# Where the second layer norm is applied, and how modulation weight rows are grouped, in an adaLN block with a long convolution

## The chip, the cores and the metric

One Trainium2 chip, one of its cores. The engines of a core run side by side, each through its own instructions in order: TensorE (PE in the profile, with its weight loads as PEld), VectorE (DVE), ScalarE (ACT), GpSimd (POOL) and SyncE (SP), whose queue issues nearly all DMAs here. The metric is the device time of one execution in microseconds; 2164.45 is the median of three runs.

## What is computed

A block on x of shape (4, 1024, 2048): a modulation vector, a layer norm with scale and shift, a long causal convolution along the last axis with a kernel from a state-space model, a gated residual, a second layer norm with its own scale and shift, and a linear layer with a low-rank update, gated again.

```python
mod = (_silu(L0_c) @ L0_wmod).reshape(L0_c.shape[0], 6, 1, -1)
sa, ca, ga, sb, cb, gb = (mod[:, 0], mod[:, 1], mod[:, 2], mod[:, 3], mod[:, 4], mod[:, 5])
ga = (2 * (ga >= 0) - 1) * jnp.maximum(jnp.abs(ga), 0.25)
gb = (2 * (gb >= 0) - 1) * jnp.maximum(jnp.abs(gb), 0.25)
h = _layernorm(x, axis=-1) * (1 + ca) + sa
x = x + ga * _L0_attn_ref(h, ...)      # causal convolution over 2048 points, plus D * h
h = _layernorm(x, axis=-1) * (1 + cb) + sb
x = x + gb * _L0_ffn_ref(h, ...)       # h W^T + bias + sum over 16 of w_e (h A_e^T) B_e^T
```

`L0_wmod` is 2048 x 12288, the FFN's W is 2048 x 2048, and A and B have rank 16 for each of 16 experts.

## The kernel before

The 4096 rows of x are worked in 32 tiles of 128 rows ("rows" r = 0 to 31 below) and, in the FFN, in 16 units u of two tiles each. All of x fits only tile by tile, so results between the stages go through HBM.

**Modulation.** The weight matrix of the modulation is cut into six sections of 2048 columns, a section into 16 weight rows of 1 MB (`mod_load`), each followed by four products of 32 output columns (`mod_mm`, L317; f32, so eight matmul records in the profile). Sections 1 and 0 run first, then section 2 (the first gate) beside rows 0 and 1; sections 4, 3 and 5 are filler later. `section` loads and multiplies one row at a time from a pool of three buffers (`WM`).

**Convolution rows.** For each row: `stats` (L497) and `conv_prep` (normalise L514, 16 transposes L535 in groups of four, scale and shift on ScalarE L538, split into two half-precision parts L546 and L547), `conv_mm` (108 half-precision products L567 with ScalarE and VectorE work at its ends, L580 to L594) and `conv_post`. `conv_post` stores the row y to HBM (`x1d`), takes the squares on ScalarE (L614), makes the reciprocal deviation (`rstd`), normalises y on VectorE (L617), transposes it in four groups of four (L623), copies each group out of PSUM on ScalarE (L624) and stores it to HBM (`n2d`, L625).

**Filler.** `PLAN` gives, for ten points in a row's products, what is taken from generators: `P` a step of `conv_post` of the row before, `N` a step of the next row's `conv_prep`, `S` a step of the filler, `T` and `F` the statistics and preparation of row r + 2. There are nine `S` in a row. The filler (`rest`) merges the low-rank update into W, in eight chunks of 15 steps (`merge`: products L443, sums L445, then seven half-precision pieces through L470 and L471), and after every `MR` = 2 merge steps takes one step of the modulation sections 4, 3 and 5. The first merge needs operands made by `prep_lora` (`lbh` and `lbl`, L418 and L419).

**FFN.** The product of a 256 x 2048 unit with a 2048 x 1024 part of W is made by a seven-product scheme of 128 x 1024 by 1024 x 512 blocks (Strassen-like; `ORDER` names the products), each as 24 matmuls (L704) on half-precision pairs. There are two passes q over the 16 units, one for each half of the columns. In pass 0 the function `left` makes the seven left operands of the next unit: it loads the transposed normalised unit from `n2d` (L652), applies scale `cb` and shift `sb` on ScalarE (L654), forms sums on VectorE (L671), casts and takes the remainder (L664, L665) and stores the pairs to HBM (`lfd`, L666); in pass 1 (q = 1) they are loaded again. `ffn_unit` evacuates the accumulators X, Y and Z between the products (copies p1, p5, p6, p7 on ScalarE L712, sums on VectorE), adds the residual from `x1d` (L719, L720) and stores the output (L751). Z is used by three products, so its copies p6 and p7 have to be made before the next one writes it.

What sets the order: the tile framework schedules instructions within the order and the priorities that the generators give; on each engine and on SP's DMA queue they then run strictly in order, and an instruction that waits keeps all behind it.

Of the kernel before, what the change touches and what calls it, by code (L numbers as in the profile page):

```python
# [24 lines left out]
P = 128  # L25
D = 2048
# [8 lines left out]
class Net:  # L35
# [254 lines left out]
    def prep_mod(self, pool):  # L290
        nc, v = self.nc, self.nc.vector
        self.small = pool.tile([P, 265], F32, tag="small", name="small")
        nc.sync.dma_start(out=self.small, in_=self.io["small"])
        c = self.small[:, 201:265].rearrange("p (b j) -> p b j", j=16)
        th = pool.tile([P, NB, 16], F32, tag="mth", name="mth")
        nc.scalar.activation(th, c, AF.Tanh, scale=0.5)
        v.tensor_scalar(th, th, 0.5, 0.5, MUL, ADD)
        v.tensor_tensor(th, th, c, MUL)
        self.sct = self.const("sct", [P, 16, 8, NB])
        v.tensor_copy(  # L300
            self.sct.rearrange("p j r b -> p r b j"),
            th.unsqueeze(1).to_broadcast([P, 8, NB, 16]),
        )
# [20 lines left out]
    def mod_column(self, pool, name, plus_one):  # L324

        nc, v = self.nc, self.nc.vector
        row = pool.tile([P, 512], F32, tag="mg0", name="mrow")
        nc.scalar.copy(row, self.modps)
        ps = self.tps.tile([P, 4, P], F32, tag="t", name="mtp")
        for c in range(4):  # L330
            nc.tensor.transpose(ps[:, c, :], row[:, ds(P * c, P)], self.ident)
        col = self.const(name, [P, NC, NB])
        src = ps.rearrange("p c (q r) -> p q c r", r=32)[:, :, :, 0:NB]
        dst = col.rearrange("p (q c) b -> p q c b", c=4)
        v.tensor_scalar(dst, src, plus_one, None, ADD)
        return col
# [270 lines left out]
    def conv_post(self, pl, r, y, sums):  # L607
        nc, v = self.nc, self.nc.vector
        STQ(nc).dma_start(out=self.x1d[r], in_=y)
        mn = pl["sm"].tile([P, 1], F32, tag="mn", name="mn")  # L610
        v.tensor_scalar(mn, sums[:, 0:1], sums[:, 1:2], -1.0 / D, ADD, MUL)
        n = pl["n"].tile([P, D], F32, tag="n", name="n2")
        sq = pl["sm"].tile([P, 1], F32, tag="sq", name="sq")
        nc.scalar.activation(n, y, AF.Square, bias=mn, accum_out=sq)  # L614
        rs = pl["sm"].tile([P, 1], F32, tag="rs2", name="rs2")
        self.rstd(pl["sm"], sq, rs, 1, "r2", 1.0 / D)
        v.tensor_scalar(n, y, mn, rs, ADD, MUL)  # L617
        yield
        for c0 in range(0, NC, 4):
            nt = pl["nt"].tile([P, 4, P], F32, tag="nt", name="nt")  # L620
            tp = self.tps.tile([P, 4, P], F32, tag="t", name="tp2")
            for k in range(4):
                nc.tensor.transpose(tp[:, k], n[:, ds(P * (c0 + k), P)], self.ident)  # L623
            nc.scalar.copy(nt, tp)  # L624
            NTQ(nc).dma_start(out=self.n2d[r // 2][:, c0 : c0 + 4, r % 2, :], in_=nt)  # L625
            yield
# [18 lines left out]
    def left(self, pl, u):  # L645
        nc, v = self.nc, self.nc.vector
        b = u // 4
        t = pl["t"].tile([P, NC, 2, P], F32, tag="t", name="gt")
        for q in range(4):
            for h in range(2):  # L650
                sl = slice(HC * h + 2 * q, HC * h + 2 * q + 2)
                nc.sync.dma_start(out=t[:, sl], in_=self.n2d[u][:, sl])  # L652
                for c in range(sl.start, sl.stop):
                    nc.scalar.activation(  # L654
                        t[:, c], t[:, c], AF.Identity,
                        bias=self.sb[:, c, b : b + 1], scale=self.cb[:, c, b : b + 1],
                    )
        a11, a12 = t[:, 0:HC, 0, :], t[:, HC:NC, 0, :]
        a21, a22 = t[:, 0:HC, 1, :], t[:, HC:NC, 1, :]
        res = {}  # L660

        def put(i, s):
            hl = pl["l"].tile([P, HC, 2, P], F16, tag="l", name="lf")
            nc.scalar.copy(hl[:, :, 0, :], s)  # L664
            v.tensor_tensor(hl[:, :, 1, :], s, hl[:, :, 0, :], SUB)  # L665
            STQ(nc).dma_start(out=self.lfd[u, i], in_=hl)  # L666
            res[i] = hl

        def comb(x, y, op, tag):
            t = pl["s"].tile([P, HC, P], F32, tag=tag, name=tag)  # L670
            v.tensor_tensor(t, x, y, op)  # L671
            return t

        put(0, a11)
        s1 = comb(a21, a22, ADD, "s1")
        put(4, s1)
        s2 = comb(s1, a11, SUB, "s2")
        put(5, s2)
        put(1, a12)
        put(6, comb(a11, a21, SUB, "s1"))  # L680
        put(2, comb(a12, s2, SUB, "s1"))
        put(3, a22)
        return res
# [9 lines left out]
    def ffn_unit(self, pl, u, q, lf, wc):  # L693
# [21 lines left out]
        xs = []  # L715
        for r in range(2):
            x = pl["o"].tile([P, 2, 512], F32, tag="o", name="xo")
            src = self.x1d[2 * u + r].rearrange("p (h n) -> p h n", h=2)[:, :, ds(512 * q, 512)]
            nc.sync.dma_start(out=x, in_=src)  # L719
            v.tensor_tensor(x, x, self.gbias, ADD)  # L720
            xs.append(x)

        def finish(r, h, cv):
            t = pl["e"].tile([P, 512], F32, tag="fin", name="fin")
            v.tensor_tensor(t, cv, self.gbt[:, h], MUL)
            v.tensor_tensor(xs[r][:, h], xs[r][:, h], t, ADD)
# [3 lines left out]
        p1 = copy("X", "p1")  # L730
        prod(4, "Y")
        p5 = copy("Y", "p5")
        prod(5, "Z")
        p6 = copy("Z", "p6")
        prod(1, "X")
        finish(0, 0, ps["X"])
        v.tensor_tensor(p6, p6, p1, ADD)
        prod(6, "Z")
# [3 lines left out]
        finish(1, 1, p7)  # L742
        prod(2, "Y")
        v.tensor_tensor(p6, p6, ps["Y"], ADD)
        finish(0, 1, p6)
        prod(3, "Z")
        v.tensor_tensor(p1, p1, ps["Z"], ADD)
        finish(1, 0, p1)
        for r in range(2):
            dst = self.io["out"][ds(256 * u + P * r, P), :].rearrange("p (h n) -> p h n", h=2)[:, :, ds(512 * q, 512)]  # L750
            STQ(nc).dma_start(out=dst, in_=xs[r])  # L751
# [5 lines left out]
MR = 2  # L757
ACC, TPS = 5, 2
PLAN = ("PNS", "N", "NS", "NT", "PS", "PS", "PS", "PS", "FS", "SS")
R0 = 3  # L760
WM, WMS = 3, 3
# [14 lines left out]
def net(ctx: ExitStack, tc: tile.TileContext, io):  # L776
# [5 lines left out]
    k.n2d = k.dram.tile([NU, P, NC, 2, P], F32, tag="n2d", name="n2d")  # L782
# [13 lines left out]
    def section(sec, pools):  # L796
        for q in range(16):
            if q == 0:
                k.mod_begin()
            k.mod_mm(k.mod_load(pools[q % len(pools)], sec, q), q)  # L800
            yield
        if sec == 0:
            k.sa = k.mod_column(msm, "sa", 0.0)
            k.hinv = k.fold_scale(msm, k.ca, k.sa, "fs1")
        elif sec == 1:
            k.ca = k.mod_column(msm, "ca", 1.0)
        elif sec == 2:
            k.gas, (k.gad,) = k.mod_gate(msm, "gad")
        elif sec == 4:
            k.cb = k.mod_column(msm, "cb", 1.0)  # L810
        elif sec == 3:
            k.sb = k.mod_column(msm, "sb", 0.0)
        else:
            _, k.gbd = k.mod_gate(msm, "gbd", io["bias"])
        yield
# [26 lines left out]
    for sec in (1, 0):  # L842
        for _ in section(sec, (wms, wmp)):
# [10 lines left out]
    for name, bufs in (("h", 2), ("n", 2), ("t", 2), ("y", 2), ("g", 1), ("nt", 2)):  # L854
        pl[name] = pool(left, "p1" + name, bufs)
    def rest():
        mods = (x for sec in (4, 3, 5) for x in section(sec, (wmp,)))
# [30 lines left out]
    def early():  # L888
        right.close()
        for name, bufs in (("w", 1), ("l", 8), ("t", 1), ("s", 1)):  # L890
            pr[name] = pool(p2, "p2" + name, bufs, "right")
        load_w(0, ORDER[0])

# [13 lines left out]
    sec = section(2, (wmp,))  # L907
# [3 lines left out]
    take(sec, 16)  # L911
# [9 lines left out]
    k.conv_late(xs.pop(0), *ys[0])  # L921
    take(k.conv_post(pl, 0, *ys[0]), 9)
    k.conv_late(xs.pop(1), *ys[1])
    post = k.conv_post(pl, 1, *ys[1])
    for r in range(2, 32):
# [6 lines left out]
        if r == LEFT0:  # L932
            while "w" not in pr:
                step()
            lf[0] = k.left(pr, 0)
# [3 lines left out]
        def tick():  # L939
            for a in next(plan):  # L940
                if a == "S":
                    step()
                elif a == "P":
                    take(post, 1)
# [8 lines left out]
        y = k.conv_mm(pl, hs.pop(r), xs.pop(r), tick, False)  # L953
        tick()
        take(post, 9)
        take(nxt, 9)
        post = k.conv_post(pl, r, *y)
        nxt = follow[0] if follow else iter(())
    take(post, 9)
    left.close()  # L960

    for name in ("v", "o", "e", "g"):
        pr[name] = pool(p2l, "p2" + name, 3 if name == "o" else 1)
    for q in range(2):
# [5 lines left out]
        for u in range(NU):  # L970
# [10 lines left out]
            k.ffn_unit(pr, u, q, lf.pop(u), wc)  # L981
            if u + 1 < NU:
                lf[u + 1] = (k.left if q == 0 else k.left_again)(pr, u + 1)
# [55 lines left out]
```

## Time and profile before

| | |
|---|---|
| three runs | 2163.26, 2164.45, 2166.11 us |
| the profiled execution: its run, its span | 2165.34 us, 2163.6 us |
| PE busy | 2080.5 us (96%) |
| DVE busy | 1355.8 us (63%) |
| ACT busy | 938.8 us (43%) |
| DMA traffic | 516.62 MB, mean 239 GB/s |
| TensorE clock granted, mean | 0.984 |

The span runs from the first to the last instruction of the program. Busy times of an engine are unions of its records; matmuls are pipelined, so a record is longer than the slot that it takes, and the distance from start to start tells more than the length. In the profile's lines `out<-in` names the tiles, L704 is line 704 of the kernel, and the last columns of a group are busy time, mean length of one and the idle time ahead of it with what ended it. Until about 110 us the kernel loads and multiplies modulation weights and builds the convolution's kernel; the rows end at 987 us, the first FFN pass at about 1577 us.

### The profile page before, as it was taken

How to read it: one execution, taken by the hardware profiler on the slowest of the kernel's cores; microseconds unless marked ns; L12 is line 12 of the kernel's file. 1: busy time of each engine (PE TensorE's matmuls, PEld its weight loads, DVE VectorE, ACT ScalarE, POOL GpSimd, SP SyncE). 2: the span in 40 equal slices, each digit the busy share in tenths (PEclk: the TensorE clock that was granted, in tenths of full speed). 3: DMA queues.
4: the chain of work that ended last, by engine and by line, in shares of the span. 5: the costliest groups of instructions: out<-in, count | busy, mean ns of one | idle time of the engine just before them, and what ended most of it. 6: DMA issues, size and time to landing. Idle time of an engine off the chain costs nothing.

```text
span 2163.6 us, 28506 instructions
## 1 busy us (share of the span) xinstructions
PE 2080.5 (96%) x11084; PEld 1019.0 (47%) x11084; DVE 1355.8 (63%) x2293; ACT 938.8 (43%) x1795; POOL 2.8 (0%) x12
## 2 busy tenths in 40 slices
PE   5698999999999999999999999999999999999998
PEld 1144555555555555564444444444444444444443
DVE  6538798889989999964665766666533333232333
ACT  1057677767776779862453535454200000000000
POOL 0000000000000000000000000000000000000000
PEclk8799999999999999999999999999999999999999
DMA  9988597888787657648756565656785544544541
GB/s 393 371 284 299 197 333 272 303 317 294 277 294 281 244 207 246 220 163 307 246 218 230 215 241 209 239 201 241 289 329 180 185 154 174 166 171 160 176 155 68
DMA packets 206497, 516.62 MB, mean 239 GB/s; under 512 B 15206, under 2 KB 80871, under 8 KB 179479
## 3 DMA queue, kind: packets, MB, share of 16 engines
q1 hardware_dynamic: 205824, 513.21, 66.3%
q8 instruction: 87, 1.43, 0.3%
q10 hardware_dynamic: 538, 1.59, 0.2%
q14 instruction: 48, 0.39, 0.1%
HBM read 325.89 MB, written 188.85 MB: 238 GB/s over the span
## 4 chain that ended last, share of the span: by engine, by line
PE 63%; DVE 15%; DMA 10%; ACT 9%; issue 2%; SPq 1%; POOL 0%; DVEq 0%; ACTq 0%
PE fZ L704 19%; PE fY L704 12%; PE fX L704 11%; PE ya L567 8%; PE yb L567 4%; PE modps L317 3%; DMA gt<-n2d 3%; PE lps L443 2%; ACT gt L654 2%; DVE lf L665 2%; PE tp L623 2%; ACT t L538 2%; ACT n L614 2%; DMA wm<-in_wmod 1%; DMA xo<-x1d 1%
## 5 line engine op out<-in xcount | busy, mean ns | idle before, releaser
L704 PEld LDWEIGHTS <-lf 128*128 128x128 f16 x5376 | 526.3, 98 | 643.0 <-issue 11.5
L704 PE MATMUL fZ<-w,lf 128*128 128x512 f16 x2304 | 514.8, 380 | 6.7 <-ACT p L712 6.7
L704 PE MATMUL fX<-w,lf 128*128 128x512 f16 x1536 | 342.6, 379 | 0.0
L704 PE MATMUL fY<-w,lf 128*128 128x512 f16 x1536 | 342.5, 379 | 0.0
L567 PEld LDWEIGHTS <-hc 128*128 128x128 f16 x2304 | 215.8, 98 | 190.7 <-issue 34.7
L720 DVE TENSOR_TENSOR xo<-xo,gb 128x1024 f32<-128x1024 f32 x64 | 78.4, 1224 | 207.0 <-DMA xo<-x1d 198.6
L538 ACT ACTIVATE t<-tp,sa,ca 128x128 f32<-128x128 f32 x512 | 199.6, 466 | 10.2 <-DVE sa L376 4.7
L654 ACT ACTIVATE gt<-gt,sb,cb 128x256 f32<-128x256 f32 x256 | 132.7, 592 | 151.7 <-DMA gt<-n2d 151.6
L567 PE MATMUL ya<-kh,hc 128*128 128x512 f16 (+3 forms) x768 | 192.6, 326 | 1.8 <-ACT qs L580 1.8
L567 PE MATMUL ya<-kh,hs 128*128 128x512 f16 (+3 forms) x768 | 193.3, 327 | 0.5 <-ACT hs L546 0.3
L567 PE MATMUL yb<-kh,hc 128*128 128x512 f16 (+3 forms) x768 | 193.0, 326 | 0.0
L317 PE MATMUL modps<-wm,sct 128*32 128x512 f32 x768 | 123.5, 687 | 32.2 <-DMA wm<-in_wmod 23.1
L567 PEld LDWEIGHTS <-hs 128*128 128x128 f16 x1152 | 107.6, 98 | 98.0 <-issue 17.7
L712 ACT COPY p<-fZ 128x512 f32<-128x512 f32 x64 | 37.3, 582 | 256.6 <-PE fZ L704 256.6
L712 ACT COPY p<-fX 128x512 f32<-128x512 f32 x32 | 18.5, 578 | 267.8 <-PE fX L704 254.9
L567 PE MATMUL ya<-kl,hs 128*128 128x512 f16 (+3 forms) x384 | 125.4, 326 | 0.0
L567 PE MATMUL yb<-kl,hc 128*128 128x512 f16 (+3 forms) x384 | 125.4, 326 | 0.0
L567 PE MATMUL ya<-kl,hc 128*128 128x512 f16 (+3 forms) x384 | 125.1, 326 | 0.0
L664 ACT CAST lf<-s 128x1024 f16<-128x1024 f32 x64 | 67.2, 1049 | 105.1 <-DVE s L671 78.7
L624 ACT COPY nt<-tp 128x512 f32<-128x512 f32 x128 | 74.9, 594 | 62.9 <-PE tp L623 43.3
L547 DVE TENSOR_TENSOR hc<-t,hc 128x512 f16<-128x512 f32 x128 | 87.5, 684 | 9.7 <-ACT hc L546 9.7
L535 PE MATMUL tp<-ident,n 128*128 128x128 f32 x512 | 79.4, 279 | 13.1 <-ACT t L538 11.6
(236 smaller groups left out, 2227.2 us busy)
## 6 DMA issues: line engine op xcount, KB each, us to landing
wm<-in_wmod SPq DMA_DIRECT2D x96, 1024.0 KB
lfd<-lf SPq DMA_DIRECT2D x112, 512.0 KB
lf<-lfd SPq DMA_DIRECT2D x112, 512.0 KB
x<-in_x SPq DMA_DIRECT2D x32, 1024.0 KB
x1d<-y SPq DMA_DIRECT2D x32, 1024.0 KB
n2d<-nt SPq DMA_DIRECT2D x128, 256.0 KB
gt<-n2d SPq DMA_DIRECT2D x128, 256.0 KB
xo<-x1d SPq DMA_DIRECT2D x64, 512.0 KB
```

The costliest lines, as they stand in the source:

```text
L317: self.last = self.nc.tensor.matmul(self.modps[32 * g : 32 * g + 32, :], self.sct[:, j].rearrange("p r b -> p (r b)"), w[:, ds(512 * g, 512)],
L443: nc.tensor.matmul(ps, la[:, x, k, h], y[:, k, osl], start=(n == 0), stop=(n == 5))
L535: nc.tensor.transpose(tp[:, k], n[:, ds(P * (c0 + k), P)], self.ident)
L538: nc.scalar.activation(t[:, k], tp[:, k], AF.Identity, bias=self.sa[:, c, b : b + 1], scale=self.ca[:, c, b : b + 1],)
L547: v.tensor_tensor(lo[:, sl], src, hi[:, sl], SUB)
L567: nc.tensor.matmul(pf[:, o:512], h, self.kf[f][z][:, ds(k0, 512 - o)], start=first, stop=(i == last and (x, z) == (1, 0)), skip_group_chec ...
L624: nc.scalar.copy(nt, tp)
L654: nc.scalar.activation(t[:, c], t[:, c], AF.Identity, bias=self.sb[:, c, b : b + 1], scale=self.cb[:, c, b : b + 1],)
L664: nc.scalar.copy(hl[:, :, 0, :], s)
L704: nc.tensor.matmul(ps[name], lf[i][:, k, x, :], wc[i][k // 4][:, k % 4, y, :], start=(first and n == 0), stop=(n == 3 * HC - 1), skip_grou ...
L712: nc.scalar.copy(t, ps[name])
L720: v.tensor_tensor(x, x, self.gbias, ADD)
```

## The change

**The layer norm.** `conv_post` no longer normalises, transposes or stores `n2d`. It keeps two numbers a row in a constant tile, `ln2`: the reciprocal deviation and minus the mean times it. Its square activation writes into the row's x tile instead of a tile of its own. In the FFN's first pass `left` loads the two rows of its unit from `x1d` (1 MB each), normalises them on ScalarE in place, transposes them on PE in eight groups of four, and applies scale and shift on ScalarE straight from PSUM. `left` is now a generator; `LPLAN` takes its steps at seven points, one after each product of `ffn_unit`: two groups of transposes after each of the first four products, the seven puts after the fifth, the loads and normalisation of the unit after next after the sixth. Unit 0 is prepared in rows 30 and 31.

**The modulation.** The last four sections that run (2, 4, 3, 5) load two weight rows and then multiply both; the pool has four buffers instead of three. The filler takes a modulation step after every four merge steps instead of two.

**Around them.** The residual is loaded and the output stored in quarters (128 x 512) instead of halves (128 x 2 x 512), with five buffers instead of three; sums of `left` are made in place; some constants move to pools that end earlier.

```diff
-    def conv_post(self, pl, r, y, sums):
+    def conv_post(self, pl, r, x, y, sums):
...
-        nc.scalar.activation(n, y, AF.Square, bias=mn, accum_out=sq)
-        rs = pl["sm"].tile([P, 1], F32, tag="rs2", name="rs2")
+        nc.scalar.activation(x, y, AF.Square, bias=mn, accum_out=sq)
+        rs = self.ln2[:, r, 1:2]
         self.rstd(pl["sm"], sq, rs, 1, "r2", 1.0 / D)
-        v.tensor_scalar(n, y, mn, rs, ADD, MUL)
-        yield
-        for c0 in range(0, NC, 4):
-            nt = pl["nt"].tile([P, 4, P], F32, tag="nt", name="nt")
-            tp = self.tps.tile([P, 4, P], F32, tag="t", name="tp2")
-            for k in range(4):
-                nc.tensor.transpose(tp[:, k], n[:, ds(P * (c0 + k), P)], self.ident)
-            nc.scalar.copy(nt, tp)
-            NTQ(nc).dma_start(out=self.n2d[r // 2][:, c0 : c0 + 4, r % 2, :], in_=nt)
-            yield
+        v.tensor_tensor(self.ln2[:, r, 0:1], mn, rs, MUL)
...
-    def left(self, pl, u):
+    def left(self, pl, u, res):
         nc, v = self.nc, self.nc.vector
         b = u // 4
+        xs = []
+        for r in range(2):
+            x = pl["x2"].tile([P, D], F32, tag=f"x2{r}", name="x2")
+            nc.sync.dma_start(out=x, in_=self.x1d[2 * u + r])
+            nc.scalar.activation(
+                x, x, AF.Identity, bias=self.ln2[:, 2 * u + r, 0:1], scale=self.ln2[:, 2 * u + r, 1:2]
+            )
+            xs.append(x)
+        yield
         t = pl["t"].tile([P, NC, 2, P], F32, tag="t", name="gt")
-        for q in range(4):
-            for h in range(2):
-                sl = slice(HC * h + 2 * q, HC * h + 2 * q + 2)
-                nc.sync.dma_start(out=t[:, sl], in_=self.n2d[u][:, sl])
-                for c in range(sl.start, sl.stop):
-                    nc.scalar.activation(
-                        t[:, c], t[:, c], AF.Identity,
-                        bias=self.sb[:, c, b : b + 1], scale=self.cb[:, c, b : b + 1],
-                    )
+        for c0 in range(0, NC, 2):
+            tp = self.tps.tile([P, 2, 2, P], F32, tag="t", name="tp2")
+            for c in range(2):
+                for r in range(2):
+                    nc.tensor.transpose(tp[:, c, r], xs[r][:, ds(P * (c0 + c), P)], self.ident)
+            for c in range(2):
+                nc.scalar.activation(
+                    t[:, c0 + c], tp[:, c], AF.Identity,
+                    bias=self.sb[:, c0 + c, b : b + 1], scale=self.cb[:, c0 + c, b : b + 1],
+                )
+            yield
...
-MR = 2
+MR = 4
-PLAN = ("PNS", "N", "NS", "NT", "PS", "PS", "PS", "PS", "FS", "SS")
+PLAN = ("PNSL", "NL", "NSL", "NTL", "SL", "SL", "SL", "SL", "FSL", "SSL")
+LPLAN = ("LL", "LL", "LL", "LL", "L", "0", "")
-WM, WMS = 3, 3
+WM, WMS = 4, 3
...
-    def section(sec, pools):
-        for q in range(16):
-            if q == 0:
-                k.mod_begin()
-            k.mod_mm(k.mod_load(pools[q % len(pools)], sec, q), q)
+    def section(sec, n, pools):
+        k.mod_begin()
+        for q in range(0, 16, n):
+            ws = [k.mod_load(pools[j % len(pools)], sec, j) for j in range(q, q + n)]
+            for j, w in enumerate(ws):
+                k.mod_mm(w, q + j)
             yield
...
-        mods = (x for sec in (4, 3, 5) for x in section(sec, (wmp,)))
+        mods = (x for sec in (4, 3, 5) for x in section(sec, 2, (wmp,)))
...
+            plan = iter(LPLAN)
+            def tick():
+                if q == 1:
+                    return
+                for a in next(plan):
+                    if a == "0":
+                        gens[0] = next_left(u + 2)
+                    take(gens[0], 1)
+            k.ffn_unit(pr, u, q, lf.pop(u), wc, tick)
```

## The prediction

> **What bounds the kernel now.** I read three views, in this order: busy time by stretches of the span, the timeline of TensorE (PE), and the groups of instructions. The stretches first (microseconds, then busy time and instruction count of PE, weight loads, VectorE, ScalarE and GpSimd, then granted clock, DMA share and GB/s):
>
> ```profile
> 200.00:300.00 100.00, 91.14 (x558) 49.22 (x559) 85.27 (x172) 77.03 (x154) 0.54 (x1) 0.97 0.73 256
> 300.00:712.00 412.00, 407.19 (x2582) 221.42 (x2581) 361.66 (x708) 298.29 (x602) 0.00 (x0) 1.00 0.82 291
> 712.00:790.00 78.00, 74.91 (x470) 44.24 (x468) 74.44 (x146) 59.66 (x124) 0.38 (x1) 1.00 0.59 206
> 790.00:987.00 197.00, 189.87 (x1234) 116.89 (x1232) 166.12 (x336) 147.70 (x324) 0.00 (x0) 1.00 0.62 213
> 987.00:1577.00 590.00, 582.77 (x2695) 263.89 (x2693) 363.18 (x408) 254.65 (x399) 0.00 (x0) 1.00 0.67 243
> 1577.00:2164.00 587.00, 580.21 (x2689) 262.84 (x2686) 186.31 (x247) 37.51 (x64) 0.00 (x0) 1.00 0.50 173
> ```
>
> PE sets the pace everywhere after 200 us. The convolution rows end at 987 us, the FFN's first pass takes 590 us and its second, with the tail, 587 us. In 300 to 712, where rows carry the weight merges and modulation rows as filler, PE is busy 98.8% and VectorE 87.8%; the 56 records of L594 there are four to a row, so 14 rows at 29.4 us, with 29.1 us of PE and 25.8 us of VectorE each. Work that is only moved on PE therefore cannot gain: what counts is work that PE loses, and idle time.
>
> **The pitch of PE's work** comes from the timeline (start, length):
>
> ```profile
> 34.46 2.78 PE L317 MATMUL modps<-wm,sct 128*32 128x512 f32 x24
> ...
> 388.77 0.38 PE L443 MATMUL lps<-lbh,lac 128*128 128x512 f16 x1
> 389.08 1.06 PE L317 MATMUL modps<-wm,sct 128*32 128x512 f32 x8
> 390.08 0.39 PE L567 MATMUL ya<-kh,hs 128*128 128x512 f16 x1
> ...
> 391.66 0.22 PE L567 MATMUL ya<-kh,hs 128*128 128x128 f16 x1
> 391.72 0.61 PE L535 MATMUL tp<-ident,n 128*128 128x128 f32 x4
> 392.16 0.38 PE L443 MATMUL lps<-lbh,lac 128*128 128x512 f16 x1
> ...
> 1306.82 5.34 PE L704 MATMUL fZ<-w,lf 128*128 128x512 f16 x24
> 1312.00 5.34 PE L704 MATMUL fY<-w,lf 128*128 128x512 f16 x24
> ```
>
> A record lasts longer than its slot, so I use starts. An FFN product is 5.18 us; a pass is 16 x 7 of them, 580.2 us, so the first pass holds 590 - 580.2 = 9.8 us of stalls. Four transposes take 392.16 - 391.72 = 0.44 us. A 512-wide half-precision product takes 0.216 us (5.18 / 24). A single modulation row takes 390.08 - 389.08 = 1.00 us plus 0.09 us ahead of it (388.77 + 0.216 to 389.08): 1.09 us. Three rows in succession take 2.78, so a further row costs (2.78 - 1.06) / 2 = 0.86 us.
>
> **The layer norm's move.** These groups go or change (count, busy us, mean ns, idle before):
>
> ```profile
> L617 DVE TENSOR_SCALAR n<-y,mn,rs 128x2048 f32<-128x2048 f32 x32 | 43.0, 1343 | 0.5
> L624 ACT COPY nt<-tp 128x512 f32<-128x512 f32 x128 | 74.9, 594 | 62.9 <-PE tp L623 43.3 <-DMA n2d<-nt 16.1 <-issue 1.1
> L654 ACT ACTIVATE gt<-gt,sb,cb 128x256 f32<-128x256 f32 x256 | 132.7, 592 | 151.7 <-DMA gt<-n2d 151.6
> L614 ACT ACTIVATE n<-y,mn 128x2048 f32<-128x2048 f32 x32 | 64.1, 2002 | 23.0 <-DVE mn L611 22.8
> ```
>
> PE: 128 groups of four transposes leave the rows (128 x 0.44 = 56 us) and 16 units x 8 groups return, 15 units of them between the products of pass 1 and unit 0's in the last rows. In the built order each of a unit's first four products is followed by eight transposes, at 0.88 us if two groups simply add. In the rows a record of eight lasts 1.14 us at 211.96 and 1.22 at 206.07, one of four 0.61: the second four cost 0.53 to 0.61, so a burst is at most 0.44 + 0.61 = 1.05 us, and none is seen below 0.88. I take 0.88, the pitch in the middle of rows: net 0, with 0 to +10 us (60 x 0.17) kept for the range. [...]
>
> VectorE loses 32 x 1.34 = 43 us and gains 32 one-column products (nearest row, L611, 0.20 us): 1.14 us a row less. ScalarE loses 75 us of copies and gains 32 full-width activations (2.0 us, the price of L614) in pass 1; its 256 modulations now read PSUM, 0.47 us (128x128 from PSUM, L538) to 0.60 (128x512 from PSUM, L624), and I take the 0.59 of today. ScalarE is then busy about 255 + 15 x 4 = 315 us of some 640 in pass 1, so this lies beside PE. Of DMAs, 128 stores of n2d and 128 loads of it go (SP issues each) and 32 loads of x1d of 1 MB come, in pass 1 two a unit; out and xo double their issues at half the size. All are issued by SP, whose count falls, and 33.5 MB less are written; both lie off the path, which is PE's.
>
> **Pass 1's stalls.** ScalarE sits 151.6 us behind gt<-n2d, and when a PSUM copy (L712) is queued behind that wait PE stalls. In the built order ScalarE's queue after a unit's fourth product (end: T) is: four modulations, a cast, the first normalisation (L643 of the new code, which waits for its 1 MB load), the copy of p7, three casts, the second normalisation, two casts. The loads are issued after the fourth burst, at T + 0.9 us. A 512 KB xo load kept the chain 5.6 to 8.7 us; taking these for 1 MB with longer rows, the first lands at T + 6.5 to T + 9.6, and p7's copy ends 2.0 + 0.6 us later, at T + 9.1 to T + 12.2. PE overwrites p7's bank with the unit's last product, at T + 0.9 + 2 x 5.18 = T + 11.3: slack of 2.2 us, or a stall of 0.9. The second normalisation ends about 6 us after that copy, T + 18 at the latest; its first user is the burst after the next unit's first product, T + 0.9 + 4 x 5.18 = T + 21.6. I take no stall in steady units (range 0 to +13, 14 x 0.9). At the change-over, units 0 and 1, I leave 4 us for the transposes and for p7, queued after six casts. 9.8 - 4: -6 us.
>
> **Modulation pairs.** A pair costs 1.09 + 0.86 = 1.95 instead of 2.18 us: 0.23 x 32 pairs = -7.5 us (24 in the filler, 8 in the gate section at 110 to 165 us, where PE has no gap over 0.4 us either). The bound is 0, if loads or order tear pairs apart; the built order keeps most whole, so I take -7.5. A fourth buffer leaves two pairs in flight, about 15 us of row time ahead.
>
> **VectorE in the filler.** Nine filler steps a row gave six merge steps and three modulation rows (two merge steps, one row); now four merge steps to a pair give 7.2 merge steps and 3.6 rows. A merge chunk has 15 steps; by L445 (8 x 0.74), L471 (7 x 1.22), four 128x1024 combinations (4 x 1.22) and 1.3 us of small ones, 20.6 us or 1.37 a step. Per row: VectorE 25.8 - 1.14 + 1.2 x 1.37 = 26.3; PE 29.1 - 1.76 (four groups) + 1.2 x 0.69 (48 products of 0.216 in 15 steps) + 0.25 (1.8 pairs of 1.95 for 3 rows of 1.09) = 28.4. VectorE is at 93%: still under PE. I add 2 us of stalls; PE's idle time in 200 to 987 (787 - 763.1 = 24 us) otherwise loses 2 us of waits behind nt.
>
> **The first merge.** PE reached L443 at 223.5 us, while the operand lbl was finished only at 226.8. Rows 0 to 4 now bring PE there up to 9 us earlier, and ScalarE, which makes that operand, sheds only nine copies (5 us). Some 3 us of the move's relief is lost: +3 (0 to +6).
>
> **The tail.** The last store is a quarter of the 1 MB row pair instead of a half: -0.5 us (0 to -1).
>
> **Sum** on the profiled span: 2163.6 - 7.5 - 6 + 2 - 2 + 3 - 0.5 = 2152.6 us. Outside the span this execution's run took 2165.34 (1.7 more); the median of the three runs is 2164.45, 0.85 above the span. I predict 2152.6 + 0.85 = 2153 us, its own range 2136 to 2160: the low end halves the 24 us of idle (-12) and drops the two losses of 3 and 2, the high end drops the pairs.
>
> **Rivals.** *VectorE becomes the bound of the filler rows.* For: 93% on average, and rows with five put steps hold 14 us of puts beside the convolution's work; against: in 712 to 790 VectorE is at 95% and the rows still flow. If it decides, VectorE is kept to the 87.8% it reached before: 26.3 / 0.878 = 30.0 us for 15 rows instead of 28.4: +24, 2177 us, slower. It decides once VectorE's share cannot pass 92%. Chance 0.17. *The copy of p7 comes late.* ScalarE's wait for x2 takes the place of its wait for gt: if the load lands 3 us after the T + 8.7 that p7 allows (11.3 - 2.6), each of 14 units stalls 3 us: +42, 2195 us, slower. For: SP issues in order, and four of the next unit's xo loads and seven lfd stores share the DMA engines; against: in the built order the loads stand ahead of six of these stores. Chance 0.10. *Moved, not gained.* The pairs save nothing and pass 1 keeps its stalls: 2153 + 7.5 + 6 = 2166, no change. Chance 0.13. The forecast has 0.60.
>
> Faster or slower means by over 0.2% (4.3 us), about what a measurement of this kernel can tell from no change. Faster 0.60, same 0.13, slower 0.27. The range, 2136 to 2178, holds the forecast, no change and VectorE's case.
>
> **What would show it.** Right: PE busy total lower by about 7 us, rows ending near 930 us, pass 1 about 640 us with bursts of 0.9 us, PE's clock 1.00 in it, modulation pairs 1.95 us apart from start to next work. Wrong: PE idle before the FFN's products behind ScalarE's p copies (late p7), PE idle in 300 to 700 behind VectorE (hc, y, we), or a clock below 1.00 in pass 1.

## The result, and the profile after

The changed kernel took 2154.53 us (median of four runs, 2150.89 to 2155.09) where the kernel before took 2165.05 (four runs, 2163.26 to 2166.11): a ratio of 0.9949, 95% interval 0.9931 to 0.9966. Measured once more beside the experiments it was 2152.35 us and 0.9935 (0.9919 to 0.9952). The forecast was 2153. The profiled execution has a span of 2149.1 us and took 2150.89, the fastest of its four.

Busy time by stretches, with the boundaries where this kernel's stages lie (microseconds, busy time and count of PE, weight loads, VectorE, ScalarE, GpSimd, then granted clock, DMA share, GB/s):

```profile
200.00:300.00 100.00, 89.75 (x538) 45.50 (x531) 86.23 (x183) 71.27 (x139) 1.06 (x1) 0.97 0.69 262
300.00:693.00 393.00, 380.56 (x2350) 199.75 (x2349) 356.63 (x722) 275.88 (x547) 0.38 (x1) 1.00 0.73 272
693.00:790.00 97.00, 95.77 (x607) 56.18 (x606) 89.33 (x205) 68.57 (x157) 0.00 (x0) 1.00 0.46 169
790.00:927.00 137.00, 134.29 (x849) 79.39 (x848) 109.42 (x232) 94.25 (x207) 0.00 (x0) 1.00 0.37 139
927.00:1563.00 636.00, 633.52 (x3172) 317.00 (x3171) 370.21 (x447) 311.21 (x440) 0.00 (x0) 1.00 0.62 226
1563.00:2149.00 586.00, 580.68 (x2691) 263.03 (x2689) 188.28 (x279) 37.51 (x64) 0.00 (x0) 1.00 0.53 174
```

The rows give way to the FFN at 927 us (before: 987). Pass 1 is 636 us long (before: 590), with 2.5 us of idle PE in it. But in 300 to 693, where filler runs, PE is busy only 96.8% of the time (before, in 300 to 712: 98.8%), and VectorE 90.7%. So the rows became shorter and yet less dense: something there costs time.

The new work of pass 1 on PE's timeline, in a steady unit, then on ScalarE's timeline at the next unit's change of the operands:

```profile
1208.69 5.34 PE L703 MATMUL fX<-w,lf 128*128 128x512 f16 x24
1213.87 1.04 PE L653 MATMUL tp<-ident,x 128*128 128x128 f32 x8
1214.74 5.34 PE L703 MATMUL fY<-w,lf 128*128 128x512 f16 x24
...
1232.03 1.04 PE L653 MATMUL tp<-ident,x 128*128 128x128 f32 x8
...
1243.26 5.34 PE L703 MATMUL fZ<-w,lf 128*128 128x512 f16 x24
```

```profile
1238.50 2.09 ACT L643 ACTIVATE x<-x,ln 128x2048 f32<-128x2048 f32 x1 [1.57 <-DMA x<-x1d]
1240.50 0.56 ACT L711 COPY p<-fZ 128x512 f32<-128x512 f32 x1
```

A burst of eight transposes takes 1214.74 - 1213.87 = 0.87 us and nothing else is lost at its edges. With T = 1232.03, the start of the unit's fourth burst (the fourth product ends there), the first normalisation starts at T + 6.5, the copy p7 ends at T + 9.0, and PE writes that bank again at T + 11.2: 2.2 us to spare. ScalarE does wait for the load there (1.57 us), but nobody waits for ScalarE.

The groups that took the place of L654 and of ScalarE's old waits:

```profile
L655 ACT ACTIVATE gt<-tp,sb,cb 128x256 f32<-128x256 f32 x256 | 125.0, 575 | 60.9 <-PE tp L653 60.9
L643 ACT ACTIVATE x<-x,ln 128x2048 f32<-128x2048 f32 x32 | 67.1, 2097 | 26.9 <-DMA x<-x1d 26.8
L703 PE MATMUL fZ<-w,lf 128*128 128x512 f16 x2304 | 513.6, 379 | 1.0 <-ACT p L711 1.0
```

ScalarE's 151.6 us of waiting for gt<-n2d are gone, and with them nearly all of PE's waits for the copies p: 1.0 us is left (6.7 before), 0.8 of it at 967 us, early in the pass.

### The profile page after: what moved, and what is told of

Same layout as the page of the kernel before. It is cut to its first block, busy times and chain, and to the rows that moved or that the text cites. A ratio compares the mean times of both kernels' runs of the same rounds, so it can differ in the third digit from the quotient of the medians.

```text
span 2149.1 us, 28402 instructions
## 1 busy us (share of the span) xinstructions
PE 2071.0 (96%) x11084; PEld 1023.3 (48%) x11084; DVE 1321.5 (61%) x2357; ACT 928.9 (43%) x1699; POOL 3.4 (0%) x12
## 4 chain that ended last, share of the span: by engine, by line
PE 63%; issue 22%; DVE 6%; ACT 2%; DMA 1%; SPq 0%; POOL 0%; POOLq 0%; DVEq 0%
PE fZ L703 22%; PE fX L703 15%; PE fY L703 15%; PE ya L567 4%; PE tp L653 3%; PE yb L567 2%; ACT x L613 1%; PE modps L317 1%; DVE y L594 1%; ACT t L538 1%; DVE st L497 1%; PE tp L535 1%; DVE hc L547 1%; DVE y L593 0%; DMA x<-x1d 0%
## 5 line engine op out<-in xcount | busy, mean ns | idle before, releaser
L721 DVE TENSOR_TENSOR xo<-xo,gb 128x512 f32<-128x512 f32 x128 | 87.8, 690 | 244.4 <-DMA xo<-x1d 232.1
L538 ACT ACTIVATE t<-tp,sa,ca 128x128 f32<-128x128 f32 x512 | 200.7, 471 | 19.3 <-PE tp L535 9.7
L655 ACT ACTIVATE gt<-tp,sb,cb 128x256 f32<-128x256 f32 x256 | 125.0, 575 | 60.9 <-PE tp L653 60.9
L317 PE MATMUL modps<-wm,sct 128*32 128x512 f32 x768 | 116.3, 679 | 29.3 <-DMA wm<-in_wmod 20.7
L726 DVE TENSOR_TENSOR fin<-fX,gb 128x512 f32<-128x512 f32 x32 | 22.1, 692 | 127.8 <-PE fX L703 127.7
L443 PE MATMUL lps<-lbh,lac 128*128 128x512 f16 x256 | 85.9, 382 | 9.2 <-ACT lbh L418 5.1
```

The lines of the kernel that those rows point to most:

```text
L317: self.last = self.nc.tensor.matmul(self.modps[32 * g : 32 * g + 32, :], self.sct[:, j].rearrange("p r b -> p (r b)"), w[:, ds(512 * g, 512)],
L443: nc.tensor.matmul(ps, la[:, x, k, h], y[:, k, osl], start=(n == 0), stop=(n == 5))
L538: nc.scalar.activation(t[:, k], tp[:, k], AF.Identity, bias=self.sa[:, c, b : b + 1], scale=self.ca[:, c, b : b + 1],)
L655: nc.scalar.activation(t[:, c0 + c], tp[:, c], AF.Identity, bias=self.sb[:, c0 + c, b : b + 1], scale=self.cb[:, c0 + c, b : b + 1],)
L721: v.tensor_tensor(x, x, self.gbias[:, h], ADD)
```

## The experiments

Each ratio is against the kernel before, run beside it on the same chip; before took 2165.75 us in the first four, 2169.76 in the next four, 2168.03 in the next three and 2168.34 in the last, so ratios are compared, not times. 0.001 is 2.17 us. "Rows end" is the start of the first FFN product in the profile.

| run | what differs | median us | ratio, 95% | span | rows end |
|---|---|---|---|---|---|
| before | | | 1 | 2163.6 | 984.5 |
| c_after | the changed kernel | 2152.35 | 0.9935 (0.9919 to 0.9952) | 2150.6 | 929.7 |
| e1_single | single modulation rows | 2146.08 | 0.9905 (0.9889 to 0.9920) | 2145.3 | 923.6 |
| e2_pairs | before with pairs | 2180.08 | 1.0062 (1.0048 to 1.0076) | 2177.0 | 995.9 |
| e5_wm3 | three weight buffers | 2157.13 | 0.9958 (0.9942 to 0.9974) | 2153.1 | 932.0 |
| e3_spread7 | seven filler steps a row | 2142.37 | 0.9879 (0.9865 to 0.9892) | 2140.7 | 919.6 |
| e7_pairs_thin | pairs at the old density | 2145.16 | 0.9890 (0.9875 to 0.9905) | 2140.8 | 919.3 |
| e8_single_dve | e1 plus 1.34 us a row on VectorE | 2161.81 | 0.9969 (0.9958 to 0.9980) | 2159.1 | 937.7 |
| e9_single_lora | e1, operands made a row earlier | 2152.47 | 0.9926 (0.9913 to 0.9940) | 2150.5 | 929.4 |
| e10_spread6 | six filler steps a row | 2140.72 | 0.9880 (0.9864 to 0.9897) | 2136.7 | 915.3 |
| e11_actnorm | first normalisation on ScalarE | 2146.30 | 0.9904 (0.9889 to 0.9919) | 2144.4 | 922.9 |
| e6_dbl | bursts doubled | 2204.07 (one run) | | 2202.3 | 929.0 |
| e12_spread7_act | e3 and e11 together | 2135.78 | 0.9846 (0.9831 to 0.9861) | 2134.5 | 912.9 |

### Which half of the change gained? The pairs undone, and the pairs alone

> The changed kernel again, beside the others on one chip. Theory A (pairs save 5 to 7 us of TensorE, the moved layer norm saves some 3 to 5 us): 2153 to 2155 us, 10 to 11 below the kernel before. Theory B (the same total, but all from the moved layer norm): the same time; only the next runs tell A from B.

e1_single takes the pairs out of the changed kernel:

```diff
-MR = 4
+MR = 2
-        mods = (x for sec in (4, 3, 5) for x in section(sec, 2, (wmp,)))
+        mods = (x for sec in (4, 3, 5) for x in section(sec, 1, (wmp,)))
-    sec = section(2, 2, (wmp,))
+    sec = section(2, 1, (wmp,))
-    take(sec, 8)
+    take(sec, 16)
```

> The changed kernel with single modulation rows (four buffers kept, one row after two merge steps). Theory A: some 24 to 32 tiling switches of 0.23 us come back, 5.5 to 7.5 us: 2160 to 2162 us. Theory B (pairs give nothing, since the filler rows are held up by VectorE): within 2 us of the changed kernel. Theory C (the pairs' denser filler costs more than the switches): 2 to 5 us faster than the changed kernel, with TensorE's idle time in 300 to 700 us down from 12.5 to about 5 us.

e2_pairs puts them alone into the kernel before (the same lines the other way round; the three buffers stay).

> The kernel before with the modulation pairs alone (three buffers, a pair after four merge steps), layer norm left where it was. Theory A: 5.5 to 7.5 us below before: 2157.5 to 2159.5 us. Theory B: no change, 2165 us. Theory C: slower than before, up to 2170 us, since VectorE has the layer norm's 1.34 us a row on top of a denser filler.

Theory A, the prediction's, fell both times; theory C came nearest, and both differences were larger than it gave. Without the pairs the changed kernel is 6.3 us faster by the medians (the two intervals just touch); with the pairs alone the kernel before is 14.3 us slower by the medians, 13.4 by the ratio and by the spans. The whole gain belongs to the rest of the change (the layer norm's move, with the fourth buffer and the quarters, which no run takes apart), and the pairs with what came with them gave a third of it back. The three buffers may play a part in e2_pairs, as the next run suggests; how much of its loss is theirs is open.

e5_wm3 sets `WM` from 4 to 3 in the changed kernel.

> The changed kernel with three weight-row buffers instead of four. Theory A: a row's load is long done when its turn comes some 15 us later, and nothing is lost: 2153 to 2156 us. Rival: the second row of each pair waits for its buffer, the pairs are torn and their 5 to 7 us are lost: about 2160 us, with gaps of TensorE in front of the second row behind a load.

It lost 4.8 us by the medians, 2.5 by the profiled spans, and its interval overlaps the changed kernel's a little, so the size is uncertain. The rival's sign, gaps ahead of rows behind a load, isn't there: PE waits 20.2 us for weight rows in all, and 21.0 with four buffers. PE's busy time is 3.5 us higher (2074.9 against 2071.4), but 2.0 of that lies in the first 200 us, in whose first half the granted clock was 0.75 instead of 0.81. So the profile doesn't show what the third buffer costs, and the size stays open.

### The pair itself, or the denser merges that came with it?

Nine steps a row held six merge steps and three modulation rows; with a pair in one step, they hold 7.2 and 3.6. e7_pairs_thin keeps the pairs and thins the filler back to 6 and 3, and e3_spread7 takes seven steps instead of nine:

```diff
                 next(mods, None)
                 yield
+                yield
```

```diff
-PLAN = ("PNSL", "NL", "NSL", "NTL", "SL", "SL", "SL", "SL", "FSL", "SSL")
+PLAN = ("PNSL", "NL", "NL", "NTL", "SL", "SL", "SL", "SL", "FSL", "SL")
```

> The changed kernel, pairs kept, with one empty step after each pair: nine steps a row again hold 6 merge steps and 3 modulation rows, as before. Theory D (density of the merge steps): 2141 to 2144 us, faster than single rows by the pairs' 5 us. Theory P (the pair itself): 2148 to 2152 us, no better than single rows, with TensorE's idle time in 300 to 700 us staying above 10 us.

> The changed kernel, pairs kept, with seven filler steps a row instead of nine: 5.6 merge steps and 2.8 modulation rows a row (changed: 7.2 and 3.6; before: 6 and 3). The run with single rows was 6 us faster than the changed kernel. Theory D (not the pairs themselves but the denser merge steps cost: VectorE evicts their products): the loss goes and the pairs' 0.23 us each stays: 2141 to 2144 us. Theory P (a pair is itself a stretch of 1.9 us in which TensorE makes nothing for VectorE and ScalarE, and these are late afterwards): it stays at 2150 to 2153 us.

Theory D holds: by their ratios to the 2165.75 us of the first four runs' before, they are at 2139.5 (e3) and 2141.9 us (e7), where the changed kernel was at 2152. PE's waits show a part of what dense merges cost. First the changed kernel (c_after), from the list of PE's waits (total us, times, longest), then e1_single, then e7_pairs_thin:

```profile
PE lps L443 <- DVE r_v L69: 2.0, 1, 2.0
PE tp L535 <- DVE n L514: 1.9, 3, 1.4
PE lps L443 <- DVE y L584: 1.8, 1, 1.8
PE yb L567 <- DVE y L593: 1.6, 2, 0.8
...
PE yb L567 <- DVE we L445: 1.4, 1, 1.4
PE lps L443 <- DVE we L445: 0.9, 1, 0.9
...
PE lps L443 <- DVE y L593: 0.5, 1, 0.5
```

```profile
PE tp L535 <- DVE n L514: 3.3, 4, 1.4
...
PE ya L567 <- DVE hs L547: 0.7, 1, 0.7
```

```profile
PE lps L443 <- DVE we L445: 3.4, 2, 1.9
...
PE tp L535 <- DVE n L514: 1.4, 1, 1.4
...
PE yb L567 <- DVE we L445: 0.5, 1, 0.5
...
PE lps L443 <- DVE y L584: 0.2, 1, 0.2
```

In the changed kernel PE waits 10.1 us for VectorE in the rows. 6.2 of it, the waits that name L584, L593 and L445, is for one of the five PSUM banks that the merges' products and the convolution's share and that VectorE empties. In e1_single it waits 4.0 us and never for such a bank, in e7_pairs_thin 5.5 us and 4.1 of it for a bank. That is 4.6 of the 9.8 us between the spans of the changed kernel and e7_pairs_thin. PE's busy time is 4.9 us higher as well (2071.4 against 2066.5), of which a stretch of 5 us at a clock of 0.66, from 645 us on, explains 1.7 (over 600 to 700 us the clock is 0.98, and 1.00 in the first profiled execution); what the rest is stays open. VectorE itself is equally busy in all three between 300 and 700 us. The changed kernel, then e7_pairs_thin, then e1_single:

```profile
300.00:700.00 400.00, 386.49 (x2378) 202.96 (x2377) 361.97 (x730) 280.45 (x557) 0.38 (x1) 1.00 0.73 270
```

```profile
300.00:700.00 400.00, 391.02 (x2444) 207.92 (x2442) 362.20 (x740) 274.52 (x556) 0.00 (x0) 1.00 0.73 269
```

```profile
300.00:700.00 400.00, 392.25 (x2428) 203.31 (x2421) 360.15 (x733) 277.15 (x565) 0.00 (x0) 1.00 0.70 262
```

VectorE stands at 90 to 91% each time, while PE's idle time is 13.5 us in the changed kernel and 9.0 and 7.8 in the others. So VectorE's share of busy time doesn't tell these kernels apart; what differs in the lists is the time for which PE stands before a bank that isn't empty yet.

The pair's own price is seen between e1 and e7, which have the same density. One row in e1_single, one pair in e7_pairs_thin, each with the product ahead of it and behind it:

```profile
255.39 0.38 PE L567 MATMUL ya<-kh,hc 128*128 128x512 f16 x1
255.70 1.06 PE L317 MATMUL modps<-wm,sct 128*32 128x512 f32 x8
256.70 0.39 PE L567 MATMUL ya<-kh,hc 128*128 128x512 f16 x1
```

```profile
255.44 0.22 PE L567 MATMUL ya<-kh,hc 128*128 128x128 f16 x1
255.59 1.92 PE L317 MATMUL modps<-wm,sct 128*32 128x512 f32 x16
257.45 0.39 PE L567 MATMUL ya<-kh,hs 128*128 128x512 f16 x1
```

A row is 1.00 + 0.09 us and a pair 1.86 + 0.09, so a pair saves 0.23, as predicted. From 115 us to the first FFN product, PE turns to modulation rows in 61 separate stretches in e1_single and in 41 in e7_pairs_thin, since some pairs are torn: 20 turns fewer are 4.6 us. PE's busy time is lower by 5.2 us (e1_single, then e7_pairs_thin), of which 1.7 is a stretch at half clock that e1_single alone has (688.9 to 692.3 us; over 600 to 700 us its clock is 0.98):

```profile
PE 2071.7 (97%) x11084; PEld 1020.8 (48%) x11084; DVE 1321.7 (62%) x2357; ACT 925.6 (43%) x1699; POOL 3.3 (0%) x12
```

```profile
PE 2066.5 (97%) x11084; PEld 1023.8 (48%) x11084; DVE 1320.2 (62%) x2357; ACT 928.3 (43%) x1699; POOL 3.3 (0%) x12
```

In the spans that is 4.5 us; by the measured ratios it is 0.0015 with overlapping intervals, so the sign of the pairs alone is read from the profiles only.

e10_spread6 goes on to six steps (the plan's first `S` taken out as well).

> The changed kernel, pairs kept, with six filler steps a row: the filler now reaches to about row 27 of 31. Theory D (VectorE, which evicts and combines the merges, is overloaded where filler is dense and has room in the rows behind it): another 1 to 4 us from the run with seven steps, ratio to before 0.986 to 0.9875. Rival: at seven steps (0.9879) the loss was all gone and nothing is left to gain: 0.987 to 0.989.

0.9880 against 0.9879: the rival. At seven steps what density cost is regained. (The profiled execution of e10_spread6, the fastest of its four, has a span 4.0 us shorter than e3_spread7's; the medians don't bear that out.)

### Is it VectorE's load that holds the rows?

If so, VectorE's lost 1.34 us a row is what the layer norm's move gained in the rows. e8_single_dve gives it back to e1_single; e11_actnorm takes another 1.34 us a row from VectorE in the changed kernel and gives ScalarE 2.0:

```diff
         v.tensor_tensor(self.ln2[:, r, 0:1], mn, rs, MUL)
+        v.tensor_scalar(x, y, mn, rs, ADD, MUL)
```

```diff
-ACTNORM = ""
+ACTNORM = "1"
```

> Single rows as before, and the normalisation that left VectorE in the rows is put back there (128x2048, 1.34 us a row; its output is not used). Theory V (the moved layer norm gained because VectorE held the rows up): some 30 x 1.34 us of VectorE work return and with them the loss in the rows without filler and the waits in the others: 2153 to 2158 us, 7 to 12 slower than single rows alone. Theory W (it gained because TensorE no longer waits for that layer norm's own tiles, n and nt): within 2 us of single rows, 2145 to 2148 us.

> The changed kernel with nine steps and pairs, and the first layer norm's normalisation (L514, 128x2048, 1.34 us a row) computed by ScalarE instead of VectorE (2.0 us a row). Theory V (VectorE holds the dense rows): the opposite of the run that put 1.34 us back, 4 to 8 us faster than the changed kernel, ratio to before 0.990 to 0.9915. Theory S (TensorE's largest wait in the rows is for ScalarE's t, so ScalarE is as near its limit as VectorE): 3 to 10 us slower than the changed kernel, ratio 0.995 to 0.998, with more wait behind t.

The times came as theory V said, both ways: +13.9 us (0.9905 to 0.9969), more than its range, and -6.7 us (0.9935 to 0.9904). But they did not come from the dense rows. The same 400 us in e8_single_dve, then in e11_actnorm:

```profile
300.00:700.00 400.00, 389.59 (x2416) 201.67 (x2415) 374.04 (x749) 275.63 (x566) 0.00 (x0) 1.00 0.72 264
```

```profile
300.00:700.00 400.00, 384.83 (x2383) 202.94 (x2382) 350.96 (x740) 312.69 (x581) 0.38 (x1) 1.00 0.73 271
```

With more work on it VectorE is busy 93.5% of the time and PE idle 10.4 us; with less, 87.7%, and PE is idle 15.2 us, more than the changed kernel's 13.5. Rows 6 to 19 take 405.9 us in e11_actnorm and 406.2 in the changed kernel (a row is counted between the ends of VectorE's last sums, L594). What VectorE lost there gained nothing; whether it would have without the 2.0 us a row that ScalarE got, these runs don't show. Of its 6.7 us e11_actnorm had gained 5.1 by the end of row 5, and 2.3 of these by the end of row 2, ahead of the filler.

The cost in e8_single_dve is as uneven. Row 3 took 43.4 us where e1 has 35.0; all later rows together lost only 4 us. Row 3 is where the first merge waits for `prep_lora`. ScalarE's timeline there, in before, in the changed kernel, in e1_single and in e8_single_dve:

```profile
194.42 2.00 ACT L405 ACTIVATE lb<-lb,lwt 128x2048 f32<-128x2048 f32 x1
...
209.34 2.00 ACT L614 ACTIVATE n<-y,mn 128x2048 f32<-128x2048 f32 x1
...
220.41 3.68 ACT L418 CAST lbh<-lb 128x2048 f16<-128x2048 f32 x2
```

```profile
194.12 2.02 ACT L405 ACTIVATE lb<-lb,lwt 128x2048 f32<-128x2048 f32 x1
...
210.88 3.68 ACT L418 CAST lbh<-lb 128x2048 f16<-128x2048 f32 x2
```

```profile
193.12 2.02 ACT L405 ACTIVATE lb<-lb,lwt 128x2048 f32<-128x2048 f32 x1
...
209.90 3.68 ACT L418 CAST lbh<-lb 128x2048 f16<-128x2048 f32 x2
```

```profile
198.83 2.00 ACT L405 ACTIVATE lb<-lb,lwt 128x2048 f32<-128x2048 f32 x1 [0.53 <-DVE lwt L399]
...
207.09 2.02 ACT L405 ACTIVATE lb<-lb,lwt 128x2048 f32<-128x2048 f32 x1
...
218.55 3.68 ACT L418 CAST lbh<-lb 128x2048 f16<-128x2048 f32 x2
```

The operand comes 9.5 us earlier in the changed kernel than in before. Put 1.34 us a row back on VectorE and it comes 8.7 us later than in e1_single, because the second L405 has slipped from 193 to 207 us: VectorE has no idle time between 184 and 198 us there, its one-column L399, which ScalarE needs, runs only at 198.66 (185.16 in e1_single), and ScalarE stands idle behind VectorE for 6.3 us from 190 to 199 us. The clock adds to it: it is 0.71 from 205 to 215 us and 0.50 from 215 to 225, where e1_single has 0.63 and 0.86. So 1.34 us a row, put into a chain of small steps across two full engines, became 8.4 us in one row.

e9_single_lora calls `prep_lora` one row earlier (`take(fill, 1)` ahead of row 2, in e1_single).

> Single rows, and the merges' operand preparation is put one row earlier in the program. Theory L (the 5.1 us that TensorE waits for lbh at 207 us are ScalarE's, which comes late to that cast): the wait goes and 3 to 5 us with it: 2141 to 2143 us. Rival: the preparation is held by its loads or by what ScalarE does for the rows there, and only pushes the rows' own work back: 2145 to 2148 us.

It lost 4.5 us (0.9905 to 0.9926), so the rival's mechanism, and more than its size. The wait for lbh went, but row 2 ended at 214.5 instead of 198.6 us, and PE's longest wait in the rows became one of 7.1 us for ScalarE's copy qs (L580): the same work of ScalarE, in front of a row instead of behind it.

### The burst's price

e6_dbl issues every transpose of units 1 to 15 twice.

> The changed kernel with every transpose of pass 1 issued twice (the second writes the same numbers over the first), so that each burst has 16 instead of 8. By the step of the prediction, 0.88 us a burst with nothing hidden: 60 x 0.87 to 0.88 is 52 to 53 us more, 2202 to 2208 us, and a granted clock of 1.00 in pass 1. Rival (a burst has a fixed part beside its eight transposes): clearly less than 52 us. [...]

Two lines of its PE timeline, and pass 1 as one stretch:

```profile
1203.16 1.91 PE L653 MATMUL tp<-ident,x 128*128 128x128 f32 x16
1204.91 5.34 PE L703 MATMUL fZ<-w,lf 128*128 128x512 f16 x24
```

```profile
929.00:1616.00 687.00, 685.27 (x3649) 369.19 (x3647) 370.72 (x447) 314.24 (x440) 0.00 (x0) 1.00 0.58 209
```

A burst of 16 takes 1.75 us, twice 0.87, and pass 1 lasts 687.5 us from first product to first product instead of 635.2: 52.3 us more, or 60 x 0.87. The clock is 1.00 throughout. So in these bursts a transpose costs 0.109 us, and no fixed part shows.

### The best of both

> Seven filler steps a row and the first normalisation on ScalarE together. Alone, against before, they gave 0.9879 and 0.9904 where the changed kernel gives 0.9935, that is some 12 and 7 us. If both relieve the same overload of VectorE in the dense rows, most of the second is already had: 0.987 to 0.989. If each takes away a wait of its own, they add: 0.984 to 0.986, about 2136 us where before is 2166.

They add: 0.9846, 2135.78 us, 1.5% below before and the best of all runs. So they don't relieve one overload of VectorE in the dense rows: e12_spread7_act is 6.0 us ahead of e3_spread7 by the end of row 3 and 6.7 where the rows end, and PE's wait for lbh at the first merge, 2.9 us in e3_spread7, is gone. PE's largest wait in the rows is then ScalarE's t (L538), 14.4 us in 13 waits, which it was before too (11.6).

## Why the prediction was right, and where it was wrong

The number was right by luck: two terms were wrong by nearly the same amount, in opposite directions. From the profiled spans of before (2163.6), e1 (2145.3), e7 (2140.8) and the changed kernel (2150.6): the layer norm's move, with the fourth buffer and the quarters, gave -18.3, pairs at the old density -4.5, and density +9.8, together -13.0; the prediction had -5.5, -7.5 and +2, together -11.0. Two profiled executions of the changed kernel differ by 1.5 us (2149.1 and 2150.6), so the parts are good to a microsecond or two. By steps:

- *Moved transposes, 0.* Right: 0.87 us a burst where 0.88 was taken, and doubled bursts cost exactly their transposes. The granted clock of pass 1 is 1.00 with bursts of 0.87 and of 1.75 us between products. A longer stretch of transposes alone was not run.
- *Pass 1's stalls, -6.* Right in kind, short in size. Between the first products of the two passes there were 592.4 us before and 636.2 after; less 580.2 of products and 60 x 0.87 of bursts, 12.2 us of losses became 3.8: -8.4. I had counted 9.8 because I let pass 1 begin at 987 us instead of at its first product, 984.5.
- *The copy of p7, the rival at 0.10.* Worked out from T, it held to 0.1 us at the near end of what was allowed: the load landed at T + 6.5, p7 ended at T + 9.0. The rival fell.
- *The first merge, +3.* This step had the wait right and its surroundings wrong. PE does wait for the operand there, 5.1 us where before has none, within the step's range. But PE was ready for its first L443 15.7 us earlier than in before (207.8 instead of 223.5), where the step had up to 9, and the operand came 9.5 us earlier, where the step let ScalarE make up only the 5 us of nine copies that it sheds. The gain ahead of the wait has no term in the sum. Row 3 went from 44.0 to 35.0 us with single rows; eight groups of transposes (3.5 us) that left it account for part, and 5.5 us is gain. VectorE's steps in the operand's chain had moved up as well (its L411, ahead of the last scaling, ran at 200.5 instead of 209.8 us).
- *VectorE in the filler, +2.* This step failed. It set VectorE's mean share, 93%, against PE's and found room; the denser merges cost 9.8 us, of which 4.6 is PE's waiting for VectorE, while VectorE's share was 90.5% in the changed kernel's dense rows and 90.6% in the thinned ones. The prediction's own rival looked for the loss in the right place, but its rule, that VectorE decides once its share cannot pass 92%, fails as well: e8_single_dve reached 93.5%, and e11_actnorm at 87.7% was no faster in the dense rows. Its +24 us was too much.
- *Waits behind nt, -2.* The later rows, with single modulation rows, gained 2.8 us beyond the transposes.
- *Modulation pairs, -7.5.* Their 0.23 us each was right, their number was not: 20 turns of PE to modulation rows fell away instead of 32, which is 4.6 us, and the spans at the old density have 4.5. Counted with the density they bring, they cost 5.3 us by the spans and 6.3 by the medians.
- *The tail, -0.5.* PE's last product to the span's end went from 6.4 to 5.4 us.

The signs named in advance nearly all came true (rows end at 927 us, pass 1 at 636, clock 1.00, PE busy lower by 9.5), and did not find the error: they were sums. The one that did was PE idle behind VectorE in 300 to 700 us, which was listed under what would prove it wrong.

## What to carry to other kernels

When an edit packs filler more densely, price the engine that empties the results as well as the one that makes them, and by the waits that it ends, not by its share of busy time: here PE stood idle 10.4 us beside VectorE at 93.5% and 15.2 us beside VectorE at 87.7%, and PE at 96 to 97% hides both. Before moving work off an engine, ask which chains of small steps run through its queue; relief there can be worth more than the instruction's length. And test a change of two parts one part at a time even when the sum comes out as forecast.

## What the runs showed of the hardware

A short wait can cost more than its length. In before, a product that began after a wait of 2.24 us ran on a lower clock (PE timeline, then the clock in that stretch):

```profile
1158.29 7.03 PE L704 MATMUL fZ<-w,lf 128*128 128x512 f16 x24 [2.24 <-ACT p L712]
1165.15 5.34 PE L704 MATMUL fY<-w,lf 128*128 128x512 f16 x24
```

```profile
1160.00:1165.00 5.00, 5.00 (x19) 1.96 (x17) 5.00 (x6) 3.33 (x4) 0.00 (x0) 0.73 0.26 105
```

It took 1165.15 - 1158.29 = 6.86 us instead of 5.18, so the wait cost 3.9 us, not 2.2. A wait of 1.64 us in the same pass and one of 2.13 in e2_pairs were followed by products of 5.17 and 5.18 us. Length alone doesn't decide it: in c_after a wait of 2.01 us that ended at 645 us was followed by a clock of 0.66 over 5 us, and in the first profiled execution of the same kernel the same wait, of the same length, by 1.00. After the changed kernel's 5.05 us wait for lbh the clock was 0.53 from 210 to 217 us. What decides beside the length, no run shows.
